# Strip runs of the value product that follow the groups of heads, in a transformer block on one core

## The chip, the cores and the metric

One core of one Trainium2 chip runs the whole kernel. The metric is device time in microseconds, as the median of several executions of the built program. Lower is better.

## The reference

The input is `x` of 2 x 1024 x 1024 (two sequences of 1024 tokens). Three sublayers follow each other, each with a layernorm without weights and a residual:

```python
x = x + 0.5 * ffn(layernorm(x))      # dense 1024x1024 + bias, 8 LoRA experts of rank 16, top 2
x = x + attn(layernorm(x))
x = x + 0.5 * ffn(layernorm(x))      # the same weights
```

The attention has 32 query heads and 8 key and value heads, each 32 wide, so four query heads share one key head; rotary positions; a causal mask; softmax; and an output projection:

```python
att   = einsum('bhgqd,bhkd->bhgqk', q, k) / sqrt(32)        # causal
probs = softmax(att)
ctx   = einsum('bhgqk,bhkd->bhgqd', probs, v)
out   = ctx @ Wo
```

All of it is in float32.

## The kernel before

The 2048 tokens are cut into 16 token tiles of 128, numbered 0 to 15; eight belong to each sequence. Token tile `t` attends to `L = t % 8 + 1` key tiles. The dense products are done in float16 halves (a high and a low part), three matmuls for each block of 128 rows. Each token tile passes four stages, written as Python generators: `a1` (first feed-forward), `a2` (keys, values, queries), `c1` (output projection, which reads the context) and `c2` (second feed-forward). The weights of `a2` and `c1` do not stay on the chip; they stream from DRAM into the three buffers `ws`, issued on SyncE's queue, and so do the transposing DMAs. `dense` (L362 to L364) holds the matmuls of all these stages: `pd<-ws` are `a2` and `c1`, `pd<-wb` and `misc<-ag` are the feed-forwards.

The attention goes through 128 pairs of a token tile and a group (four query heads with one key head). The token tiles come in the order 0 to 7, 9 to 15, and tile 8 (`LATE`) at the very end. For each pair:

- `unit_s1` computes the scores (L571) for each key tile, takes the row maximum on VectorE (L588), writes it into the queries as extra columns (L598, L599), and loads the queries again, transposed, by a DMA on SyncE's queue (`qt_load`, L554). This runs some pairs ahead (`LOOK`).
- `unit_s2` computes the transposed scores (L686) for each key tile, the exponential on ScalarE (L692) into a buffer `p32`, and for the diagonal key tile the mask on GpSimd (L694). Each such result is a unit, which it hands to `av_add`.
- `av_add` gathers units into a batch. A batch holds up to `BATCH` = 4 key tiles of one pair, and it is emitted once two further units (`SKEW`) are there.
- `av_batch` emits the batch: a strip run. For each unit there are 8 matmuls in float32: four heads, each with a stationary operand 32 columns wide at its own quarter of the array, once with the values (`va`) and once with ones, which gives the softmax's denominator. Each of the 8 appears twice in the profile. The result is in one PSUM buffer `av` (one buffer in all). At the last key tile of the pair the sums are copied out on ScalarE (L640, `o`), inverted and multiplied on VectorE (L642, L647), cast to the high half on ScalarE (L648), and the low half is taken on GpSimd (L649). High and low half are column blocks of the context tile, which `c1` reads as its stationary operand, blocks 0 to 7 in order.

So before, a pair with one to four key tiles is one run, and one with five to eight is a run of four and a run of the rest. The lines of the batching are

```python
if not pend or len(pend[-1][3]) == BATCH or pend[-1][0:2] != (t, g):
    pend.append((t, g, L, []))
```

A step for each token tile goes through its eight pairs and advances the dense stages of other tiles between the units, by sizes that are written out. The order in which instructions stand on each engine in the end is decided when the program is built, by a list scheduler with priorities. Within a run each matmul is tied to the one before it (`issue_after` with high priority), so nothing comes between them.

Of the kernel before, what the change touches and what calls it, by code (L numbers as in the profile page):

```python
# [9 lines left out]
FP = mybir.dt.float32  # L10
# [3 lines left out]
ALU = mybir.AluOpType  # L14
# [3 lines left out]
NH, NKV, DH, GRP = 32, 8, 32, 4  # L18
E, R = 8, 16
P = 128  # L20
KB = D // P
# [7 lines left out]
ATT = [t for t in range(NT) if t != LATE] + [LATE]  # L29
LOOK = [6, 6, 4, 4, 3, 3, 3, 3]  # L30
BATCH = 4
SKEW = 2
AHEAD = 5
NEARLY = 3
# [5 lines left out]
def kernel(  # L40
# [16 lines left out]
    nc = tc.nc  # L57
# [18 lines left out]
    p_av = ctx.enter_context(tc.tile_pool(name="p_av", bufs=1, space=bass.MemoryType.PSUM))  # L76
# [525 lines left out]
    pend = deque()  # L602
    ready = {}
    avt = [None]
# [12 lines left out]

    def av_batch():

        t, g, L, us = pend.popleft()  # L620
        if us[0][0] == 0:
            avt[0] = p_av.tile([P, 2, P], FP, name="av")
        av = avt[0]
        prev = None
        for n, (j, p32) in enumerate(reversed(us)):
            for i, w in enumerate((VA[t - t % TPB + j][:, g, :], ones)):
                for h in range(GRP):
                    rows = slice(h * DH, (h + 1) * DH)
                    with ExitStack() as st:
                        if prev is not None:  # L630
                            st.enter_context(tc.high_priority())
                            st.enter_context(tc.issue_after(prev.ins))
                        prev = nc.tensor.matmul(  # L633
                            av[rows, i, :], lhsT=w, rhs=p32[:, h, :],
                            start=(us[0][0] == 0 and n == 0 and i == 0), stop=(us[-1][0] == L - 1 and n == len(us) - 1),
                            skip_group_check=True, tile_position=(0, h * DH),
                        )
        if us[-1][0] == L - 1:
            o = pp.tile([P, 2, P], FP, name="o", bufs=2)
            nc.scalar.copy(o, av)  # L640
            rc = pp.tile([P, P], FP, name="rc", bufs=1)
            nc.vector.reciprocal(rc, o[:, 1, :])  # L642
            if t not in CTX:
                CTX[t] = Context()
            c = CTX[t]
            o2 = pp.tile([P, P], FP, name="o2", bufs=2)
            nc.vector.tensor_tensor(o2, o[:, 0, :], rc, ALU.mult)  # L647
            nc.scalar.copy(c.high(g), o2)  # L648
            nc.gpsimd.tensor_tensor(c.low(g), o2, c.high(g), ALU.subtract)  # L649
            if g == NKV - 1:  # L650
                CT[t] = CTX.pop(t)

    def av_add(t, g, j, L, p32):

        if not pend or len(pend[-1][3]) == BATCH or pend[-1][0:2] != (t, g):
            pend.append((t, g, L, []))
        pend[-1][3].append((j, p32))
        after = 0
        while len(pend) > 1:
            after = sum(len(b[3]) for b in list(pend)[1:])  # L660
            if after < SKEW:
                break
            av_batch()
# [15 lines left out]
    def unit_s2(t, g):  # L679
        b0 = t - t % TPB  # L680
        L = t - b0 + 1
        q = Ts.pop(("q2", t, g))
        cs = S["cs", g // 4]
        for j in range(L):
            ps = p_s2.tile([P, GRP, P], FP, name="s2")
            ins = nc.tensor.matmul(  # L686
                ps.rearrange("p h k -> p (h k)"), lhsT=KT[b0 + j][:, g, :],
                rhs=q.rearrange("p h k -> p (h k)"), start=True, stop=True,
            )
            s2_ins.append(ins.ins)  # L690
            p32 = pp.tile([P, GRP, P], FP, name="p32", bufs=8)
            nc.scalar.activation(p32, ps, AF.Exp, scale=cs)  # L692
            if j == L - 1:
                nc.gpsimd.affine_select(  # L694
                    out=p32, in_=p32, compare_op=ALU.is_ge, fill=0.0, base=0,
                    pattern=[[0, GRP], [1, P]], channel_multiplier=-1,
                )
            av_add(t, g, j, L, p32)
            yield

    def stage_c1(t):
        while t not in CT:
            av_batch()
        tt = CT.pop(t)
        xt = xts[t]
        for n in range(2):
            ps = p_dense.tile([P, 512], FP, name="pd")
            yield from dense_streamed(ps, tt, 3 + n)
            c = bass.ts(n, 512)
            nc.vector.scalar_tensor_tensor(xt[:, c], ps, S["uo", n], xt[:, c], ALU.mult, ALU.add)  # L710
            if n == 0:
                yield True
        Ts["x3", t] = layernorm(xt)
        yield True
# [94 lines left out]
    pp = ctx.enter_context(tc.tile_pool(name="pp", bufs=2, reuse_waits="tile"))  # L809
# [5 lines left out]
    def flush(_):  # L815
        while pend:
            av_batch()
        yield True
# [68 lines left out]
    def step(s):  # L887
# [26 lines left out]
        for g in range(NKV):  # L914
            u = pos + g + 1 + LOOK[t % TPB]
            if s == LATE - 1:
                u = min(u, LATE * NKV)
            if s == NT - 1 and g == 3:
                QS[LATE] = qst[LATE % 2]
                nc.sync.dma_start(out=QS[LATE], in_=late["q"])  # L920
            if u < len(units) and units[u][0] != t and s < NT - 1:
                while s != LATE - 1 and ready.get(units[u][0], 0) < (1 if units[u][1] < 4 else 2):
                    next(dn)
                    done += 1
            s1 = look(u)
            for _ in unit_s2(t, g):
                next(s1, None)
                slot += 1
                while done < npieces * slot / nslots:
                    next(dn, None)  # L930
                    done += 1
            for _ in s1:
                pass
# [73 lines left out]
```

## Time and profile before

| | us |
|---|---|
| median of 4 runs | 1524.83 |
| lowest, highest | 1523.23, 1526.64 |
| the profiled execution | 1523.23 |
| its span, first to last instruction | 1521.5 |

| engine | busy us | instructions |
|---|---|---|
| TensorE matmuls (PE) | 1428.3 | 16596 |
| TensorE weight loads (PEld) | 833.3 | 16596 |
| VectorE (DVE) | 1066.8 | 2396 |
| ScalarE (ACT) | 691.6 | 1280 |
| GpSimd (POOL) | 497.3 | 711 |

| stretch (us from the start) | transposed scores of token tiles |
|---|---|
| 152 to 307 | 0, 1, 2 (one to three key tiles) |
| 307 to 795 | 3 to 7 (four to eight) |
| 848 to 985 | 9, 10 (two, three) |
| 986 to 1442 | 11 to 15 (four to eight) |
| 1443 to 1470 | 8 (one) |

The first 150 us prepare the weights and begin the first feed-forwards. A row of the profile names the line, the engine, the operation and the tiles: `av<-p,va` writes `av` and reads `p32` and `va`. The matmuls overlap in the array, so their durations are longer than the distance of their starts; the distance is what counts where PE is the bound.

### The profile page before, as it was taken

To read this page: it belongs to the slowest core of one execution; us is meant where nothing else is said; L and a number is where in the kernel's file an instruction comes from. 1 tells how busy PE (TensorE), PEld (TensorE's weight loads), DVE (VectorE), ACT (ScalarE), POOL (GpSimd) and SP (SyncE) were. 2 spreads that over 40 slices of the span, in tenths; PEclk is the share of its full clock that TensorE was granted. 3 is DMA by queue.
4 is the path that set the end of the run, shared out by engine and by line. 5 is a ranking of instruction groups with operands and counts; after the bars stand their busy time and mean duration, and the time that the engine had idled before them with its cause. 6 is when DMAs were issued, how large, how long until landed. Compare 5 with 4: busy or idle time off the path is not lost.

```text
span 1521.5 us, 39480 instructions
## 1 busy us (share of the span) xinstructions
PE 1428.3 (94%) x16596; PEld 833.3 (55%) x16596; DVE 1066.8 (70%) x2396; ACT 691.6 (45%) x1280; POOL 497.3 (33%) x711
## 2 busy tenths in 40 slices
PE   3877989899999999999999898999999999999998
PEld 1433445556556566666654454555556566566543
DVE  6878666867768577776663756867877577776653
ACT  7444334544444454454550333444444455565520
POOL 3453342624324133232231433434333132231231
PEclk9998999999999999999999999999999999999999
DMA  9877796958494753646547769668594653663461
GB/s 279 290 204 203 166 276 188 225 148 239 103 249 90 211 170 78 237 114 146 185 119 245 187 157 251 187 178 228 96 266 87 201 169 78 209 140 78 123 190 43
DMA packets 297186, 267.57 MB, mean 176 GB/s; under 512 B 262576, under 2 KB 265648, under 8 KB 276528
## 3 DMA queue, kind: packets, MB, share of 16 engines
q1 hardware_dynamic: 293456, 252.47, 61.5%
q10 hardware_dynamic: 3552, 12.58, 2.2%
q8 instruction: 130, 2.13, 0.6%
q14 instruction: 48, 0.39, 0.1%
HBM read 181.63 MB, written 20.45 MB: 133 GB/s over the span
## 4 chain that ended last, share of the span: by engine, by line
PE 75%; DVE 10%; DMA 8%; issue 2%; POOL 2%; ACT 1%; SPq 1%; DVEq 0%; POOLq 0%; ACTq 0%
PE av L633 15%; PE pd L362 13%; PE pd L363 13%; PE pd L364 13%; PE s L571 8%; PE s L686 7%; DMA qt<-qst 3%; DMA ws<-wstr 2%; DVE ws L196 2%; DVE mx L588 1%; DVE hl L315 1%; DMA xt<-in_x_dram 1%; DMA tt<-hl 1%; PE pd L444 1%; PE pd L446 1%
## 5 line engine op out<-in xcount | busy, mean ns | idle before, releaser
L692 ACT ACTIVATE p<-s,cs 128x512 f32<-128x512 f32 x576 | 379.5, 687 | 281.8 <-PE s L686 278.9
L588 DVE TENSOR_REDUCE mx<-s 128x4 f32<-128x512 f32 x480 | 316.0, 676 | 162.6 <-PE s L571 149.6
L633 PE MATMUL av<-p,va 128*32 128x128 f32 x4608 | 237.0, 278 | 1.7 <-POOL p L694 1.0
L362 PE MATMUL pd<-ws,tt 128*128 128x512 f16 x592 | 226.3, 382 | 12.4 <-DMA ws<-wstr 8.5
L633 PE MATMUL av<-p,ones 128*32 128x128 f32 x4608 | 232.3, 273 | 0.0
L363 PE MATMUL pd<-ws,tt 128*128 128x512 f16 x592 | 225.9, 382 | 0.0
L364 PE MATMUL pd<-ws,tt 128*128 128x512 f16 x592 | 225.0, 381 | 0.0
L571 PE MATMUL s<-kts,qt 96*128 96x128 f16 x2304 | 200.0, 220 | 12.7 <-DMA qt<-qst 7.7
L686 PE MATMUL s<-qt,kts 128*128 128x512 f16 x576 | 201.1, 381 | 9.5 <-DMA qt<-qst 7.2
L363 PEld LDWEIGHTS <-tt 128*128 128x128 f16 x1360 | 134.2, 99 | 134.3 <-issue 16.9
L362 PEld LDWEIGHTS <-tt 128*128 128x128 f16 x1360 | 134.1, 99 | 134.2 <-DMA tt<-hl 12.1
L364 PEld LDWEIGHTS <-tt 128*128 128x128 f16 x1360 | 134.1, 99 | 128.8 <-issue 7.2
L571 PEld LDWEIGHTS <-qt 96*128 96x128 f16 x2304 | 151.4, 98 | 96.8 <-issue 35.7
L362 PE MATMUL pd<-wb,tt 128*128 128x512 f16 x512 | 195.5, 382 | 7.0 <-DMA tt<-hl 3.6
L363 PE MATMUL pd<-wb,tt 128*128 128x512 f16 x512 | 195.0, 381 | 1.5 <-DVE wb L196 1.5
L364 PE MATMUL pd<-wb,tt 128*128 128x512 f16 x512 | 195.0, 381 | 0.0
L633 PEld LDWEIGHTS av<-p,va 128*32 128x32 f32 x4608 | 122.5, 110 | 68.7 <-issue 58.9
L642 DVE RECIPROCAL rc<-o 128x128 f32<-128x128 f32 x128 | 121.1, 946 | 49.7 <-ACT o L640 49.5
L649 POOL TENSOR_TENSOR tt<-o,tt 128x128 f16<-128x128 f32 x128 | 55.7, 435 | 296.0 <-ACT tt L648 295.9
L694 POOL TENSOR_SCALAR_AFFINE_SELECT p<-p 128x512 f32<-128x512 f32 x128 | 84.5, 661 | 199.0 <-ACT p L692 199.0
L633 PEld LDWEIGHTS av<-p,ones 128*32 128x32 f32 x4608 | 138.4, 110 | 0.1
L583 POOL TENSOR_SCALAR_AFFINE_SELECT sm<-sm 128x512 f32<-128x512 f32 x96 | 62.9, 655 | 207.0 <-ACT sm L582 206.8
(175 smaller groups left out, 1798.1 us busy)
## 6 DMA issues: line engine op xcount, KB each, us to landing
ws<-wstr SPq DMA_DIRECT2D x148, 1024.0 KB, 5.6
wstr<-ws ACTq DMA_DIRECT2D x9, 1024.0 KB, 5.6
xt<-in_x_dram SPq DMA_DIRECT2D x16, 512.0 KB, 3.9
out_dram<-xt SPq DMA_DIRECT2D x15, 512.0 KB, 2.9
qt<-qst SPq DMA_TRANSPOSE x256, 3.0
ws<-in_wb_dram SPq DMA_DIRECT2D x2, 1024.0 KB, 8.8
qst<-in_wb_dram SPq DMA_DIRECT2D x2, 1024.0 KB, 7.5
st<-in_wo_dram SPq DMA_DIRECT2D x2, 1024.0 KB, 10.3
```

The lines of the kernel that those rows point to most:

```text
L362: nc.tensor.matmul(ps, lhsT=th, rhs=wh, start=(k == 0), stop=False)
L363: nc.tensor.matmul(ps, lhsT=th, rhs=wl, start=False, stop=False)
L364: nc.tensor.matmul(ps, lhsT=tl, rhs=wh, start=False, stop=(last and k == KB - 1))
L571: nc.tensor.matmul(ps[:, h, :], lhsT=q[0 : 3 * DH, h, :], rhs=KT[b0 + j][0 : 3 * DH, g, :], start=(not pem or h == 0), stop=not pem,)
L583: nc.gpsimd.affine_select(out=sm, in_=sm, compare_op=ALU.is_ge, fill=-3.0e38, base=0, pattern=[[0, GRP], [-1, P]], channel_multiplier=1,)
L588: nc.vector.tensor_reduce(mx[:, j, :], ps, AX.X, ALU.max)
L633: prev = nc.tensor.matmul(av[rows, i, :], lhsT=w, rhs=p32[:, h, :], start=(us[0][0] == 0 and n == 0 and i == 0), stop=(us[-1][0] == L - 1 ...
L642: nc.vector.reciprocal(rc, o[:, 1, :])
L649: nc.gpsimd.tensor_tensor(c.low(g), o2, c.high(g), ALU.subtract)
L686: ins = nc.tensor.matmul(ps.rearrange("p h k -> p (h k)"), lhsT=KT[b0 + j][:, g, :], rhs=q.rearrange("p h k -> p (h k)"), start=True, stop ...
L692: nc.scalar.activation(p32, ps, AF.Exp, scale=cs)
L694: nc.gpsimd.affine_select(out=p32, in_=p32, compare_op=ALU.is_ge, fill=0.0, base=0, pattern=[[0, GRP], [1, P]], channel_multiplier=-1,)
```

## The change

Batches may now hold units of two groups. With `L` up to `PAIRED` = 3 key tiles, an even group and the odd one after it go into one batch (two, four or six units), and both accumulate in one PSUM buffer, which is now one bank of 2 x 2 x 128 float32 columns. With `L` of 4 to `LONG` = 6, all key tiles of a group go into one batch. With 7 and 8 it stays at 4 and the rest. The evacuation is done once for each pair of groups where they share the bank: its instructions are then twice as wide. The buffers `o` and `rc` are twice as wide, `o2` is twice as wide with one buffer in place of two, and `p32` has ten buffers in place of eight.

```diff
+LONG = 6
+PAIRED = 3
...
-        t, g, L, us = pend.popleft()
-        if us[0][0] == 0:
-            avt[0] = p_av.tile([P, 2, P], FP, name="av")
+        t, g0, L, us = pend.popleft()
+        if us[0][1] == 0:
+            avt[0] = p_av.tile([P, 2, 2, P], FP, name="av")
         av = avt[0]
+        n = us[-1][0] - g0 + 1
+        last = us[-1][1] == L - 1
         prev = None
-        for n, (j, p32) in enumerate(reversed(us)):
+        for g, j, p32 in reversed(us):
             for i, w in enumerate((VA[t - t % TPB + j][:, g, :], ones)):
...
-                            av[rows, i, :], lhsT=w, rhs=p32[:, h, :],
-                            start=(us[0][0] == 0 and n == 0 and i == 0), stop=(us[-1][0] == L - 1 and n == len(us) - 1),
+                            av[rows, g - g0, i, :], lhsT=w, rhs=p32[:, h, :],
+                            start=(us[0][1] == 0 and (g, j) == us[-1][0:2] and i == 0), stop=(last and (g, j) == us[0][0:2]),
...
-        if us[-1][0] == L - 1:
-            o = pp.tile([P, 2, P], FP, name="o", bufs=2)
-            nc.scalar.copy(o, av)
-            rc = pp.tile([P, P], FP, name="rc", bufs=1)
-            nc.vector.reciprocal(rc, o[:, 1, :])
+        if last:
+            o = pp.tile([P, 2, 2, P], FP, name="o", bufs=2)[:, 0:n]
+            nc.scalar.copy(o, av[:, 0:n])
+            rc = pp.tile([P, 2, P], FP, name="rc", bufs=1)[:, 0:n]
+            nc.vector.reciprocal(rc, o[:, :, 1, :])
...
-            o2 = pp.tile([P, P], FP, name="o2", bufs=2)
-            nc.vector.tensor_tensor(o2, o[:, 0, :], rc, ALU.mult)
-            nc.scalar.copy(c.high(g), o2)
-            nc.gpsimd.tensor_tensor(c.low(g), o2, c.high(g), ALU.subtract)
-            if g == NKV - 1:
+            o2 = pp.tile([P, 2, P], FP, name="o2", bufs=1)[:, 0:n]
+            nc.vector.tensor_tensor(o2, o[:, :, 0, :], rc, ALU.mult)
+            hi, lo = c.tt[:, g0 : g0 + n, :], c.tt[:, KB + g0 : KB + g0 + n, :]
+            nc.scalar.copy(hi, o2)
+            nc.gpsimd.tensor_tensor(lo, o2, hi, ALU.subtract)
+            if us[-1][0] == NKV - 1:
                 CT[t] = CTX.pop(t)
...
-        if not pend or len(pend[-1][3]) == BATCH or pend[-1][0:2] != (t, g):
+        two = L <= PAIRED
+        fresh = not pend or (not two if pend[-1][0:2] != (t, g) else len(pend[-1][3]) == (BATCH if L > LONG else L))
+        if pend and two:
+            fresh = pend[-1][0] != t or (g % 2 == 0 and j == 0)
+        if fresh:
             pend.append((t, g, L, []))
-        pend[-1][3].append((j, p32))
+        pend[-1][3].append((g, j, p32))
...
-            p32 = pp.tile([P, GRP, P], FP, name="p32", bufs=8)
+            p32 = pp.tile([P, GRP, P], FP, name="p32", bufs=10)
```

## The prediction

> **What bounds the kernel now.** I read the page first: engine shares, then the chain.
>
> ```profile
> PE 1428.3 (94%) x16596; PEld 833.3 (55%) x16596; DVE 1066.8 (70%) x2396; ACT 691.6 (45%) x1280; POOL 497.3 (33%) x711
> ...
> PE 75%; DVE 10%; DMA 8%; issue 2%; POOL 2%; ACT 1%; SPq 1%; DVEq 0%; POOLq 0%; ACTq 0%
> ...
> L633 PE MATMUL av<-p,va 128*32 128x128 f32 x4608 | 237.0, 278 | 1.7 <-POOL p L694 1.0
> ```
>
> PE is the bound, and its strip matmuls (L633) wait for almost nothing. But the 94% is a mean, so I cut the span into stretches (length; busy us of PE, PEld, DVE, ACT and POOL with instructions; clock; DMA share; GB/s).
>
> ```profile
> 187.00:245.00 58.00, 51.17 (x506) 26.70 (x506) 37.51 (x97) 22.53 (x48) 20.84 (x31) 0.97 0.88 239
> 310.00:795.00 485.00, 484.70 (x6372) 296.83 (x6371) 347.97 (x760) 235.72 (x434) 146.86 (x210) 1.00 0.59 163
> 912.00:985.00 73.00, 66.38 (x709) 37.11 (x708) 54.34 (x113) 31.25 (x63) 29.99 (x40) 0.98 0.87 228
> 985.00:1424.00 439.00, 435.43 (x5928) 269.89 (x5927) 319.26 (x681) 221.03 (x406) 131.98 (x191) 1.00 0.59 155
> ```
>
> From 310 to 795 us, and nearly so from 985 to 1424, PE has no gap: there a saved PE nanosecond is a saved nanosecond. In the stretches of the short tokens (one to three key tiles) it lacks 7 us of 58 or 73, at 87% busy DMA: there waits set part of the pace.
>
> Then the timeline of PE around a strip run, first of one unit, then of four (start, duration).
>
> ```profile
> 1458.16 0.38 PE L686 MATMUL s<-qt,kts 128*128 128x512 f16 x1
> 1458.47 0.42 PE L633 MATMUL av<-p,va 128*32 128x128 f32 x8
> 1458.72 0.40 PE L633 MATMUL av<-p,ones 128*32 128x128 f32 x8
> 1459.05 0.40 PE L571 MATMUL s<-kts,qt 96*128 96x128 f16 x4
> ...
> 699.91 0.38 PE L364 MATMUL pd<-wb,tt 128*128 128x512 f16 x1
> 700.22 0.43 PE L633 MATMUL av<-p,va 128*32 128x128 f32 x8
> ...
> 702.10 0.40 PE L571 MATMUL s<-kts,qt 96*128 96x128 f16 x4
> ```
>
> Wide matmul to wide matmul, 0.89 us with one unit between, 2.19 with four. Three units cost 1.30, so one costs 0.434 to 0.437. Neighbouring wide matmuls start 0.216 apart. So 0.89 - 0.437 - 0.216 = 0.234 us belongs to no matmul: some 0.09 at the head and 0.14 at the tail, the price of entering and leaving the strip shape, the same for one unit as for four.
>
> **Part 1: fewer runs.** In the built programs' PE order I counted stretches of L633. Before 191: 32 of one unit, 32 of two, 30 of three, 96 of four, 1 of six. After 136: 8 of two, 16 of three, 72 of four, 16 of five, 24 of six. The matmuls are as many as before. 55 runs x 0.234 = 12.8 us of PE time. By place: 32 of the 55 belong to the tokens of five and six key tiles (16 per batch), which lie in the two stretches without gaps: 32 x 0.234 = 7.5 us, wholly on the path. The other 23, 5.4 us, belong to the tokens of one to three key tiles: 11 or 12 at 152 to 307 us, 7 or 8 at 848 to 985, 4 at 1443 to 1486.
>
> **Part 2: the wider evacuation.** 24 fewer each of L640, L642, L647, L648 and L649 (ACT and DVE lose 48 instructions each, POOL 24), hidden behind PE. But a pair's chain is longer. One group takes 371 + 946 + 348 + 297 + 435 ns = 2.4 us, with handovers about 2.8. For two groups the doubled DVE, ACT-cast and POOL rows and the nearest copy row (687, an ACT read of 128x512) give 0.69 + 1.89 + 0.70 + 0.59 + 0.87 = 4.7, with handovers 5.1; if width cost nothing it stays 2.8. I take 5, since reciprocal and subtract are long for their size. Who waits is the output projection of the same token, by the PE work that the new order puts between a token's last run and the first use of its context block 6: token 1 15 us, token 2 25, token 9 12, token 10 29, token 8 9: covered. Token 0 has 0.1 us: PE waits 4 to 5 us there. Before it waited at that spot too (0.80 for L648, then 1.72 for a weight load):
>
> ```profile
> 191.38 0.39 PE L362 MATMUL pd<-ws,tt 128*128 128x512 f16 x1 [0.80 <-ACT tt L648]
> ...
> 194.00 0.58 PE L362 MATMUL pd<-ws,tt 128*128 128x512 f16 x1 [1.72 <-DMA ws<-wstr]
> 194.38 0.63 PE L363 MATMUL pd<-ws,tt 128*128 128x512 f16 x1
> ```
>
> The last two rows show what a wait can cost beyond itself: the next starts are 0.38 to 0.43 apart, not 0.216, and the windows view has the clock at 0.50 for 193.84 to 197.25, that is 1.7 us lost. The clock is at 0.50 also at 876.5 and 934.5 (3.4 us each) and 286.0 (6.8 us); after the short wait at 1490.83 (0.63 us) it isn't.
>
> [...]
>
> So token 0's spot goes from 2.5 + 1.7 to about 4 + 1.7: +1.5. If the copy and reciprocal widen for nothing it is -2.
>
> **Part 3: the order around.** The scheduler moves wide work too. I summed PE rows between a group's last score matmul (L571) and its first transposed one (L686), between which lie the row maximum, two small DVE writes and a transposing DMA. In the trace the shortest such distance without a wait for the transposed queries is 5.1 us, and many take 8. After the change token 1's groups 1 to 3 have 2.6, 3.5 and 4.0 us of PE work (before 6.3, 9.8, 12.1) and token 9's group 2 has 3.1 (before 4.6). Token 0's wait above lies ahead of the first and swallows it; I take +1.5 for the rest of token 1 (a paired run also stands only 0.5 us behind its last scores) and +2 for token 9. Token 2 gains room (group 6: 5.7 to 9.6), where before had waits of 1.2 and 1.8: -1. Bounds for the part: -3 (all old waits gone) to +8 (each a full wait with its half clock).
>
> **Part 4: the end.** Token 8 runs last. Before, its output projection was through at 1490.0 and its second feed-forward began at 1503.79:
>
> ```profile
> 1489.60 0.59 PE L364 MATMUL pd<-ws,tt 128*128 128x512 f16 x2
> 1490.83 0.38 PE L362 MATMUL pd<-wb,tt 128*128 128x512 f16 x1 [0.63 <-DVE xt L710]
> ...
> 1503.79 0.23 PE L362 MATMUL misc<-ag,tt 128*128 128x136 f16 x1 [1.15 <-DMA tt<-hl]
> ```
>
> The 13.8 us between are a serial layernorm, split and transposing DMA, under 11.6 us of PE work of token 15. The new order leaves 7.8 us of work there. The chain shortens by one L710 (0.7) and one L335 (0.64), since the first half is done earlier: 12.5. So PE waits 4.7 us and may then run 3.4 us at half clock (1.7 more), against about 3.0 us of waits from 1483 on before. Net +3.4; bounds 0 (some of the old waits recur in neither) to +5.
>
> **Part 5: edits at nothing.** Ten weight buffers for eight: at most 9 units lie between first exponential and run's end in the new order (before 7 of 8), so no exponential waits for one. The single o2 buffer makes L647 wait for L649 of the run before; runs lie at least 1.6 us apart, mostly 5, and L649 follows L647 in about 1.2. The doubled reciprocal holds DVE 0.9 us longer in 24 places, ahead of L588, which frees the score banks; PE waited for L588 3.7 us in all before. I take 0; if each showed it would be 24 x 0.9 = 22. The one bank: PE waited for L640 0.6 us in the whole run.
>
> [...]
>
> **Sum.** -12.8 + 1.5 (token 0) + 1.5 (token 1) + 2 (token 9) - 1 (token 2) + 3.4 (end) = -5.4. The profiled execution took 1523.23 us (span 1521.5): 1517.8. It was the fastest of the four runs, 1.6 under the median 1524.83: 1519.4. As the old clock losses at 193.84 and 286.0 may go, I round down to 1519.
>
> **Rivals.** *The runs' time comes back whole* (no new waits, since the waits are on DMA and the stretches re-settle): 1524.83 - 12.8 = 1512. For it: the waits of before at 152 to 307 are as many as I add. Against: the 7.8 us left at the end are in the order. *Slower*: the pairs starve PE at the short tokens. Place: the 24 paired runs and the projections and scores behind them. Price: a wait of 2.3 us plus 1.7 of half clock, 4 each. From four such on it eats the 12.8, and six beyond my list give -5.4 + 24 = +18.6, so 1543; three give +6.6, 1531. Against: PE waited for L694 1.0 and for L640 0.6 us in all. *Nothing to measure* (0.2%, 3 us, is what a measurement of this kernel can tell): three or more of the 23 short-token gains lost and a hard end, 1522 to 1528. That the runs do not merge is ruled out by the order.
>
> **How the numbers follow.** Forecast (1514 to 1521.8) 0.56; whole gain (1510 to 1514) 0.18; nothing 0.15; slower 0.11. Faster is the first two: 0.74. The range takes in the whole gain's middle and the no-change case up to 1525.5, leaving out about 0.2.
>
> **What would show it.** In the profile after: PE busy less by 10 to 13 us; stretches of tokens 4, 5, 12 and 13 each shorter by 1.9; token 0's projection waiting for L648 or L649 about 4 us; an idle row of 4 to 5 us before the last L362 misc. Wrong: if the gap-free stretches don't shorten by 7.5 us in sum, if the half clock lasts beyond 25 us in all after 150 us, or if waits for L588 or L640 show in tens of us.

## The result and the profile after

The change made the kernel slower by a little: median 1527.23 us (53 runs) beside 1524.55 us for the kernel before (79 runs). The ratio is 1.0018, 95% interval 1.0012 to 1.0024, that is +2.7 us (1.8 to 3.7). The forecast was 1519 us, and "faster" at 0.74. The profiled execution took 1527.07 us, its span 1525.2; the one of the kernel before, 1523.23 us, was 1.3 us under its median. Three executions among those of the experiments took 1679, 3737 and 4266 us, and the ratios leave them out.

Lines after the change stand two to nine higher: L633 is now L637, L571 L573, L588 L590, L648 L653, L686 L695, L692 L701, L694 L703.

The page after: engine shares, the chain, and the row of the strip matmuls with its idle time.

```profile
PE 1423.5 (93%) x16596; PEld 845.5 (55%) x16596; DVE 1056.2 (69%) x2348; ACT 683.1 (45%) x1232; POOL 495.5 (32%) x687
...
PE 64%; DVE 14%; DMA 9%; POOL 5%; issue 4%; ACT 2%; SPq 1%; DVEq 0%; POOLq 0%; ACTq 0%
...
L637 PE MATMUL av<-p,va 128*32 128x128 f32 x4608 | 237.2, 278 | 5.6 <-POOL p L703 5.6
```

PE's busy time fell, but its share of the chain fell from 75% to 64%: more of the end is set by chains through VectorE, DMAs and GpSimd. The strip runs, which had waited 1.7 us in all, now wait 5.6 us for the mask.

The windows view, cut where the transposed scores of the first token of each stretch begin (tokens 0 to 2, 3 to 7, 9 and 10, 11 to 15, then 8 with the end; columns as in the prediction).

```profile
152.70:314.40 161.70, 142.62 (x1474) 82.22 (x1474) 110.11 (x245) 60.52 (x109) 59.88 (x78) 0.95 0.74 201
314.40:853.40 539.00, 533.79 (x6657) 323.90 (x6655) 368.96 (x807) 243.43 (x451) 164.11 (x225) 1.00 0.63 170
853.40:983.30 129.90, 120.93 (x1207) 68.48 (x1205) 94.02 (x219) 52.13 (x93) 48.58 (x66) 0.97 0.78 204
983.30:1444.60 461.30, 449.17 (x6233) 283.24 (x6231) 328.35 (x706) 229.61 (x422) 136.86 (x194) 1.00 0.57 153
1444.60:1521.00 76.40, 70.62 (x529) 35.99 (x526) 35.35 (x83) 14.57 (x30) 19.31 (x24) 0.98 0.39 111
```

The same cut of the kernel before and of one experiment (the changed kernel without its runs of six, told below), as length and PE's idle time (length minus PE busy):

| tokens | before | after | after, no runs of six |
|---|---|---|---|
| 0 to 2 | 155.0, 15.3 | 161.7, 19.1 | 160.9, 20.7 |
| 3 to 7 | 540.8, 1.4 | 539.0, 5.2 | 536.4, 1.9 |
| 9, 10 | 137.3, 11.8 | 129.9, 9.0 | 130.9, 8.9 |
| 11 to 15 | 457.6, 6.8 | 461.3, 12.1 | 459.3, 7.8 |
| 8 and the end | 73.9, 3.5 | 76.4, 5.8 | 75.8, 5.3 |
| sum | 1364.6, 38.9 | 1368.3, 51.2 | 1363.3, 44.6 |

Some work moves across the cuts between short and long tokens of a sequence (64 matmuls more in the first row). By whole sequences (rows one and two, three and four) the matmul counts agree within 4, and the first became 4.9 us longer, the second 3.7 shorter, the end 2.5 longer. The key is the two rows of the long tokens together, about 998 us with 8.2 us idle before. PE busy fell there by 7.2 us; some 2 us of this is work that now lies outside the cuts (16 matmuls fewer; an estimate from the distances of such matmuls' starts, 0.06 to 0.22 us). So about 5 us of the 7.5 forecast were saved. Idle time rose by 9.1.

Token 0's projection and the end, from PE's timeline, each with the windows row of the clock behind it (the column before the last two).

```profile
202.74 0.61 PE L364 MATMUL pd<-ws,tt 128*128 128x512 f16 x1 [4.31 <-ACT tt L653]
...
202.40:205.80 3.40, 3.06 (x14) 1.68 (x15) 0.28 (x1) 1.55 (x3) 0.89 (x2) 0.50 0.53 107
```

```profile
1506.02 0.23 PE L364 MATMUL misc<-ag,tt 128*128 128x136 f16 x1 [4.95 <-DMA tt<-hl]
...
1506.25:1509.65 3.40, 3.40 (x27) 2.75 (x24) 0.53 (x4) 0.57 (x2) 0.00 (x0) 0.50 0.07 29
```

These two waits came where and as long as the prediction put them, each with 3.4 us of half clock behind it (1.5 and 1.7 us lost).

New are small waits inside the stretches that had none. PE's waits from 480 to 620 us (tokens 5 and early 6; us in total, times, longest), first the changed kernel, then the one without runs of six:

```profile
PE pd L364 <- DMA ws<-wstr: 1.0, 2, 0.7
PE s L573 <- DVE mx L590: 0.8, 2, 0.6
PE s L573 <- DMA qt<-qst: 0.7, 1, 0.7
PE s L695 <- ACT p L701: 0.4, 2, 0.2
PE av L637 <- POOL p L703: 0.4, 1, 0.4
```

```profile
PE s L573 <- DVE mx L590: 0.6, 1, 0.6
```

What such a wait looks like, at the border of tokens 5 and 6: the timeline of PE and of ScalarE.

```profile
573.20 0.43 PE L637 MATMUL av<-p,va 128*32 128x128 f32 x8
...
575.96 0.62 PE L573 MATMUL s<-kts,qt 96*128 96x128 f16 x8
576.41 0.60 PE L695 MATMUL s<-qt,kts 128*128 128x512 f16 x2
...
578.36 0.38 PE L573 MATMUL s<-kts,qt 96*128 96x128 f16 x4 [0.17 <-DVE mx L590]
578.97 0.38 PE L695 MATMUL s<-qt,kts 128*128 128x512 f16 x1 [0.23 <-ACT p L701]
```

```profile
576.83 1.24 ACT L355 ACTIVATE xn<-xt,nb,rs 128x1024 f32<-128x1024 f32 x1 [3.17 <-DVE nb L350]
577.98 0.35 ACT L644 COPY o<-av 128x256 f32<-128x256 f32 x1
578.23 1.27 ACT L701 ACTIVATE p<-s,cs 128x512 f32<-128x512 f32 x2
```

For 2.76 us PE does nothing but the run, and no new score reaches ScalarE. Then PE gives out two score tiles and two transposed ones at once. But ScalarE's 3.17 us of idle time end with a layernorm row (L355) that waited for its statistics from VectorE (L350). This row of 1.24 us stands ahead in ScalarE's order; then come the copy of the run's sums and, only at 578.23, the two exponentials. There are two buffers for each kind of score, so PE has to wait. These rows do not tell the two causes apart, the bunch of scores and the layernorm row ahead of it: without runs of six, ScalarE at this border does two exponentials (577.50) before its layernorm row (579.22). At 1257 to 1262 us, the same border in the second sequence, the same rows recur.

### The profile page after: what moved, and what is told of

Read it like the earlier page. It is cut to its first block, busy times and chain, and to the rows that moved or that the text cites. A ratio compares the mean times of both kernels' runs of the same rounds, so it can differ in the third digit from the quotient of the medians.

```text
span 1525.2 us, 39320 instructions
## 1 busy us (share of the span) xinstructions
PE 1423.5 (93%) x16596; PEld 845.5 (55%) x16596; DVE 1056.2 (69%) x2348; ACT 683.1 (45%) x1232; POOL 495.5 (32%) x687
## 4 chain that ended last, share of the span: by engine, by line
PE 64%; DVE 14%; DMA 9%; POOL 5%; issue 4%; ACT 2%; SPq 1%; DVEq 0%; POOLq 0%; ACTq 0%
PE av L637 13%; PE pd L364 12%; PE pd L365 12%; PE pd L366 11%; PE s L573 7%; PE s L695 6%; DMA qt<-qst 3%; DMA ws<-wstr 3%; DVE mx L590 3%; DVE ws L198 2%; DVE hl L317 1%; POOL xt L401 1%; DVE bst L337 1%; DMA tt<-hl 1%; DVE rc L646 1%
## 5 line engine op out<-in xcount | busy, mean ns | idle before, releaser
L701 ACT ACTIVATE p<-s,cs 128x512 f32<-128x512 f32 x576 | 377.2, 688 | 250.3 <-PE s L695 246.7
L590 DVE TENSOR_REDUCE mx<-s 128x4 f32<-128x512 f32 x480 | 318.6, 678 | 215.6 <-PE s L573 193.6
L637 PE MATMUL av<-p,va 128*32 128x128 f32 x4608 | 237.2, 278 | 5.6 <-POOL p L703 5.6
L637 PE MATMUL av<-p,ones 128*32 128x128 f32 x4608 | 233.9, 275 | 0.0
L573 PE MATMUL s<-kts,qt 96*128 96x128 f16 x2304 | 199.4, 220 | 16.8 <-DMA qt<-qst 8.3
L365 PEld LDWEIGHTS <-tt 128*128 128x128 f16 x1360 | 134.4, 99 | 136.5 <-issue 12.1
L573 PEld LDWEIGHTS <-qt 96*128 96x128 f16 x2304 | 153.0, 98 | 102.5 <-issue 35.3
L695 PE MATMUL s<-qt,kts 128*128 128x512 f16 x576 | 195.9, 381 | 4.6 <-ACT p L701 2.3
L637 PEld LDWEIGHTS av<-p,va 128*32 128x32 f32 x4608 | 128.0, 110 | 48.7 <-issue 34.3
L703 POOL TENSOR_SCALAR_AFFINE_SELECT p<-p 128x512 f32<-128x512 f32 x128 | 85.7, 670 | 197.8 <-ACT p L701 197.6
L637 PEld LDWEIGHTS av<-p,ones 128*32 128x32 f32 x4608 | 139.4, 111 | 0.2
L646 DVE RECIPROCAL rc<-o 128x128 f32<-128x128 f32 (+1 forms) x104 | 117.4, 1129 | 29.2 <-ACT o L644 29.1
L654 POOL TENSOR_TENSOR tt<-o,tt 128x128 f16<-128x128 f32 (+1 forms) x104 | 55.1, 530 | 253.6 <-ACT tt L653 253.5
```

Of the source, the lines that this page charges most:

```text
L365: nc.tensor.matmul(ps, lhsT=th, rhs=wl, start=False, stop=False)
L573: nc.tensor.matmul(ps[:, h, :], lhsT=q[0 : 3 * DH, h, :], rhs=KT[b0 + j][0 : 3 * DH, g, :], start=(not pem or h == 0), stop=not pem,)
L590: nc.vector.tensor_reduce(mx[:, j, :], ps, AX.X, ALU.max)
L637: prev = nc.tensor.matmul(av[rows, g - g0, i, :], lhsT=w, rhs=p32[:, h, :], start=(us[0][1] == 0 and (g, j) == us[-1][0:2] and i == 0), st ...
L646: nc.vector.reciprocal(rc, o[:, :, 1, :])
L654: nc.gpsimd.tensor_tensor(lo, o2, hi, ALU.subtract)
```

## The experiments

All but one are cut from the changed kernel. The diffs show what differs from it. Each ratio is to the kernel before, run beside it. Differences in us are (ratio - 1) x 1524.5; the interval of each is about ±2 us, ±3 for the runs of three and of seven.

**Runs of five alone, and runs of five and six, without pairs.**

```diff
-LONG = 6
-PAIRED = 3
+LONG = 5
+PAIRED = 0
```

> Only the tokens of five key tiles change: all five in one run in place of 4 + 1; no pairs. 175 runs in place of 191. Theory A (a run's entry and exit, 0.234 us, is really saved, and what the change lost are new waits at the tokens of one, two and six key tiles): 16 x 0.234 = 3.7 us less than before, and no waits over 0.1 us in the stretches of tokens 4 and 12. Theory B (the saving is never collected, because PE then waits for something else everywhere): 0. Theory C (any change of the order moves the time by a few us at random): anywhere from -4 to +4.

Measured: 1520.85 us, ratio 0.9981 (0.9966 to 0.9996), -2.9 us: near theory A, though theory C's span holds it too. PE waits for nothing at token 4 and 0.3 us at token 12 (0.7 before). The trace, of the slowest of the 12 executions (1525.97 us), doesn't show the gain: its two rows of the long tokens take 998.4 us as before, with 3.1 us less PE busy and 3.1 more idle.

```diff
-PAIRED = 3
+PAIRED = 0
```

> Runs of five and of six, no pairs. 159 runs. Theory A: -7.5 from 32 runs, plus the waits of the changed kernel in the stretches of tokens 5 and 13 (3.9 and 4.9 us there, none before): about +1 against before, and about 4.5 us slower than the kernel with runs of five alone. Theory B: 0 and no difference between the two. Theory C: no pattern.

Measured: 1528.42 us, ratio 1.0028 (1.0016 to 1.0040), +4.3 us. The only difference between the two is that 16 pairs have one run of six in place of four and two. That saves 16 runs and costs 7 us more. By the row prices it should have saved 3.7; with the waits already seen in the changed kernel, theory A had put it 4.5 us above the fives. One chain of it, from GpSimd's and PE's timelines:

```profile
545.23 3.50 POOL L401 TENSOR_TENSOR xt<-xt,bb 128x512 f32<-128x512 f32 x2
548.68 0.64 POOL L585 TENSOR_SCALAR_AFFINE_SELECT sm<-sm 128x512 f32<-128x512 f32 x1
...
556.64 0.39 PE L695 MATMUL s<-qt,kts 128*128 128x512 f16 x1 [1.71 <-DMA qt<-qst]
```

A mask of scores stood behind two bias additions; the row maximum, the DMA of the queries and the transposed scores behind it came late. This suggested GpSimd's queue as the cause, which the last pair of runs tries.

**Pairs alone, and without those of the tokens of one key tile.**

```diff
-LONG = 6
+LONG = 4
```

> Pairs of groups for tokens of one to three key tiles, nothing else (runs of up to four as before otherwise). 168 runs. Theory A: -5.4 from 23 runs, plus the new waits of the changed kernel at tokens 0, 1 and 8 (token 0's projection 4.3, half clock 5 more, the end 3.3, less what token 9 and 2 gain): +4 to +6, so 0 to +2 us in all; the waits of 4 to 5 us for L653 near 200 us and for the transposed split near 1500 us stand in the trace. Theory B: 0. Theory C: no pattern, and these two waits not at those places.

Measured: 1526.55 us, ratio 1.0008 (0.9996 to 1.0020), +1.2 us, as expected; 0 (theory B) is inside the interval too. The two waits stand in the trace where theory A put them (4.3 us for L653, 4.9 before the last feed-forward), which speaks against C.

```diff
-LONG = 6
+LONG = 4
...
-        two = L <= PAIRED
+        two = 2 <= L <= PAIRED
```

> Pairs only for tokens of two and three key tiles; tokens 0 and 8 as before. 176 runs. Theory A: -3.5 from 15 runs; the wait near 200 us for token 0's context and the 5 us wait before the last feed-forward are gone, so -1 to -4 against before, and 1 to 5 us faster than the kernel with all pairs. Theory B: 0. Theory C: no pattern.

Measured: 1529.83 us, ratio 1.0030 (1.0018 to 1.0042), +4.6 us: a miss. The wait for token 0's context fell from 4.3 to 0.8 us and the one before the last feed-forward from 4.9 to 1.1, both as expected, but at token 2 new waits stand that neither kernel had. From PE's timeline, and from its waits between 260 and 300 us:

```profile
270.63 1.03 PE L573 MATMUL s<-kts,qt 96*128 96x128 f16 x8 [3.27 <-DMA qt<-qst]
```

```profile
PE s L695 <- DMA qt<-qst: 4.4, 1, 4.4
```

Undoing the two parts I had priced as losses made the kernel slower: near the short tokens what an edit does is not its own price, but where the whole order lands.

**Runs of five, with pairs in some tokens.**

```diff
-LONG = 6
+LONG = 5
...
-        two = L <= PAIRED
+        two = t in (9, 10)
```

> Runs of five, and pairs only for tokens 9 and 10. 167 runs in place of 191. Theory A, put together from the stretches (each stretch's loss or gain belongs to its own tokens): -3.7 from the fives; tokens 9 and 10 took 137.3 us before and 130.2 with pairs, token 11 after them 2.4 more, so -4.7; in all about -8 against before, with no wait for token 0's context and no 5 us wait at the end. Rival (the short tokens' waits are settled by the whole order, and not by their own stretch): no better than the fives alone, -3.

Measured: 1519.22 us, ratio 0.9963 (0.9948 to 0.9978), -5.6 us, the middle between the two expectations. It is the fastest version found and beats both kernels.

```diff
-LONG = 6
+LONG = 5
...
-        two = L <= PAIRED
+        two = L <= PAIRED and t != LATE
```

> Fives, and pairs for all short tokens but the last one (token 8). 156 runs. Theory A: the fives alone gave -2.9 to -4, all pairs +1.5, and the end without pairs gets 2.5 to 3.3 back: -4 to -6 against before, and the wait before the last feed-forward 1.2 us again instead of 5. Token 0's wait of 4.3 us stays. Rival: the end is settled elsewhere, -2.

Measured: 1521.30 us, ratio 0.9984 (0.9968 to 1.0000), -2.4 us: the rival's value, though both waits are as theory A said (4.3 us at token 0, 1.1 before the last feed-forward). By the medians the pairs of tokens 0 to 2 take back 3.2 us of the 5.6, about as much as the ±3 us of such a difference; the two traces do not show it (1363.9 us from token 0's first transposed score to the end, 1365.0 without these pairs).

**The changed kernel without runs of six.**

```diff
-LONG = 6
+LONG = 5
```

> The changed kernel with the sixes cut to four and two as before, the pairs and the fives kept. If the parts add up: the fives alone gave -4.2 us and the pairs alone +1.2, so -3 us, 1521 to 1522 beside 1524.5 (ratio 0.998). Rival, the short tokens' stretches are settled by the whole order and not by the part: anything from -6 to +2 us.

Measured: 1523.92 us, ratio 0.9995 (0.9981 to 1.0009), -0.8 us, inside the rival's span and 2.2 us above the sum, which lies just outside the interval. It is the last column of the table above. Against it the runs of six in the changed kernel cost 3.5 us; in the two stretches of long tokens they save 3.0 us of PE time and bring 7.6 us of idle time. (The trace without them is of its fastest execution, 1520.25 us.)

**Is it the length of the run?** The pairs of six key tiles as two runs of three (as many runs as before, another order), and the pairs of seven as one run of seven (no pairs in both, fives kept):

```diff
-PAIRED = 3
+PAIRED = 0
...
-len(pend[-1][3]) == (BATCH if L > LONG else L))
+len(pend[-1][3]) == {5: 5, 6: 3}.get(L, BATCH))
```

> Fives, and the six key tiles in two runs of three instead of four and two: as many runs as the kernel with fives alone (175), another order. If it is the length of the run that brings the waits at the tokens of six (it can't be parted, so the scores behind it come in a bunch): no waits over 0.5 us in their stretches and the same time as with the fives alone (-3 against before). If any other order at these tokens brings waits: 3 to 5 us of them in each of the two stretches, and 4 to 8 us slower than the fives alone.

Measured: 1526.86 us, ratio 1.0013 (0.9993 to 1.0032), +2.0 us. That is 4.9 us above the fives, inside the 4 to 8 of "any other order", and speaks against the length alone. The same kernel once more, for its trace:

> The kernel of the run before it (five key tiles in one run of five, six in two runs of three), once more, for its waits. If any other order at the tokens of six key tiles brings waits, the waits of TensorE in the stretches of tokens 5 and 13 come to 3 us or more in each (none in the kernel before, 3.2 and 3.9 with one run of six). If only the length of the run does it, they are below 1 us in each.

Measured: 1525.07 us, one execution. Its waits are neither below 1 us nor above 3 in both. Between a token's first transposed score and the next token's, PE waits 0 us at token 5 and 2.0 at token 13, where the fives alone already wait 1.4; with runs of six it is 2.3 and 3.0 in the changed kernel. So in these traces the waits of token 5 come only with the run of six; at token 13 the order brings some by itself. From token 0's first transposed score to the end it takes 1368.5 us, like the fives alone (1369.4, their slowest execution) and the kernel before (1369.1). Why the median of this kernel lies some 5 us above that of the fives stays open.

```diff
-PAIRED = 3
+PAIRED = 0
...
-len(pend[-1][3]) == (BATCH if L > LONG else L))
+len(pend[-1][3]) == {5: 5, 7: 7}.get(L, BATCH))
...
-p32 = pp.tile([P, GRP, P], FP, name="p32", bufs=10)
+p32 = pp.tile([P, GRP, P], FP, name="p32", bufs=11)
```

(`o`, `rc` and `o2` are one group wide here.)

> Fives, and the seven key tiles in one run (eleven weight buffers): 159 runs, 3.7 us less of entries and exits than the fives alone. In the built order the PE work between a group's last score and its transposed score falls to 3.5 to 6 us at token 14 (8 to 11 before) and 7 to 12 at token 6. Theory of the long run: waits of 1 to 2 us for the transposed queries at token 14 and 6 in a good part of the groups, 6 to 12 us in all, so 2 to 8 us slower than the fives alone. If only six is unlucky: 3.7 us faster than the fives alone.

Measured: 1542.46 us, ratio 1.0124 (1.0102 to 1.0146), +18.9 us, that is 21.8 above the fives: the expectation was right in sign, far too small in size. From its waits of PE:

```profile
PE s L695 <- DMA qt<-qst: 23.3, 15, 3.7
```

Before, that wait was 7.2 us in six times, all at tokens 0 to 2. Here it is 8.0 us there, 3.7 at token 6, 3.3 at token 7, none at token 14 and 8.2 at token 15: so one of the two tokens forecast, and the two of eight key tiles that follow them. In the stretches of the long tokens it is nil with runs of five and in the changed kernel, 4.7 us with runs of six and no pairs, and 15.2 here.

**Is it GpSimd's queue?** Both kernels with the bias addition cut to 16 of each 512 columns, which leaves most of the bias out:

```diff
-            c = bass.ts(n, 512)
+            c = slice(512 * n, 512 * n + 16)
             nc.gpsimd.tensor_tensor(xt[:, c], xt[:, c], bb[:, c], ALU.add)
```

> The kernel before with the bias addition on GpSimd cut to 16 of each 512 columns (so most of the bias is left out): 64 additions of 1.7 us shrink to about 0.15 us each, and the order on the engines stays nearly as it was. Theory: GpSimd's queue, in which a mask or a copy of the row maximum stands behind two additions of 3.4 us, is what turns the new order's shorter distances into waits. Then this kernel gains little, 0 to 6 us, since the order before had few such waits (POOL p 1.0 us, row maximum 3.7 us).

Measured on the kernel before: 1511.38 us, ratio 0.9918 (0.9903 to 0.9933), -12.5 us, twice what was expected. The shrunk additions take 0.47 us in the mean, not 0.15. In the traces, which are 9.2 us apart, nearly all of it lies ahead of token 0, which begins at 143.4 us in place of 152.4:

```profile
143.40:1507.80 1364.40, 1327.05 (x16073) 782.81 (x16071) 902.54 (x2094) 609.96 (x1148) 367.00 (x608) 0.99 0.63 168
```

From there on it takes 1364.4 us beside 1364.6 (both cut 4.4 to 4.5 us before the end): in these traces, cutting GpSimd's additions gained nothing in the part that the change touches.

> The changed kernel with the bias addition on GpSimd cut in the same way. Theory (GpSimd's queue makes the waits): it gains 8 to 13 us and comes to lie 5 to 9 us under the kernel before with the same cut, about as I had first predicted. Rival (the distances in the order alone, whatever stands in GpSimd's queue): it gains what the other gains, and stays within 3 us of it or above.

Measured on the changed kernel: 1516.90 us, ratio 0.9943 (0.9926 to 0.9959), -8.7 us. Against the changed kernel it gained 11.4 us, inside the theory's 8 to 13, but the other gained 12.5; what tells them apart is where it lies, and that is 3.8 us above the kernel before with the same cut, as the rival said. The theory that GpSimd's queue makes the loss falls. With most of the additions gone, PE waits for weights and for queries instead, which were 8.6 and 7.7 us in the kernel before with the same cut (PE's waits in the whole run):

```profile
PE pd L364 <- DMA ws<-wstr: 15.5, 10, 3.2
PE s L695 <- DMA qt<-qst: 10.3, 4, 7.3
```

## Why the prediction was wrong

The experiments split the change into parts. A measured term is the difference of two kernels' ratios to the kernel before, good to about ±3 us (±2 for fives and sixes). The terms form one chain of kernels, so their sum is the whole by construction. The column of the traces is the same difference in one profiled execution each, from token 0's first transposed score to the end (1369.1 us in the kernel before).

| part | runs saved | forecast us | measured us | in the traces | from |
|---|---|---|---|---|---|
| fives | 16 | -3.7 | -2.9 | +0.3 | fives alone |
| sixes | 16 | -3.7 | +3.5 | +4.6 | changed kernel against the one without sixes |
| pairs of 9, 10 | 8 | +0.1 | -2.7 | -4.3 | fives with those pairs against fives alone |
| pairs of 0 to 2 | 11 | -0.6 | +3.2 | -1.2 | all pairs but token 8's against pairs of 9, 10 |
| pairs of 8 | 4 | +2.5 | +1.6 | +4.0 | all pairs against all but token 8's |
| sum | 55 | -5.4 | +2.7 | +3.4 | |

The sixes are the part that stands clear: without pairs they cost 7.2 us by the medians and 5.2 in the traces.

**The step that failed** is in Part 1: "32 x 0.234 = 7.5 us, wholly on the path". It took the gap-free stretches as a place where a saved PE nanosecond is a saved nanosecond. PE did save time there, but a gap-free stretch says only that no wait showed with the order as it was, not that the other engines had room to spare. By the medians the sixteen fives kept most of their gain (-2.9 us, between -0.6 and -5.2; their one trace shows none). The sixteen sixes missed theirs by 7.2 us; the sum was wrong by 8.1, and the errors of the other parts nearly cancel. A run of six holds PE for 2.76 us, in which no score comes out; then scores come out in a bunch, with two buffers for each kind, and ScalarE and VectorE serve them in turn. Most of the waits that are new are 0.2 to 0.7 us long, and they have different releasers: late row maximum, exponential, mask, queries, weights. That merging four and two into six brings the loss is shown by two pairs of kernels whose code differs in nothing else (+3.5 and +7.2 us). Why it does is argued from the rows: which part is the run's length and which the order that the scheduler makes around it is only partly settled, by the runs of three (another order alone: 4.9 us above the fives) and of seven.

**Part 3** had the wrong waits. For tokens 0 to 2 I took +0.5 (+1.5 - 1) and looked only at the way from scores to transposed scores. The waits for the queries, which I priced, in fact shrank from 7.7 to 2.0 us between 152 and 314 us. Two others came, one for streamed weights and one at the mask of the units themselves, from PE's and GpSimd's timelines:

```profile
186.06 0.61 PE L364 MATMUL pd<-ws,tt 128*128 128x512 f16 x1 [5.02 <-DMA ws<-wstr]
```

```profile
290.41 2.49 POOL L401 TENSOR_TENSOR xt<-xt,bb 128x512 f32<-128x512 f32 x2
292.85 1.62 POOL L703 TENSOR_SCALAR_AFFINE_SELECT p<-p 128x512 f32<-128x512 f32 x1
...
295.47 0.68 POOL L703 TENSOR_SCALAR_AFFINE_SELECT p<-p 128x512 f32<-128x512 f32 x1
...
296.21 0.66 PE L637 MATMUL av<-p,va 128*32 128x128 f32 x8 [3.40 <-POOL p L703]
```

The weights' three loads were issued from 176.80 us on, behind four loads of queries; before, single ones went out at 171.88 and 175.81, and PE waited 3.1 us there in two pieces. The four kernels with pairs at tokens 0 to 2 and the whole bias addition all have this wait in one piece (2.9 to 5.0 us). The half clock behind it in the changed kernel (185.3 to 188.7) stands in no term.

A run takes its units in reverse, the masked one first, so in a pair of token 2 one late mask holds back six units. The clock is at half from 294.5 to 301.3, so that the run behind the wait takes 5.31 us in place of 2.76: 6 us lost at one place. It is not 6 us more than before: token 2 had 6.8 us of half clock before too and 6.1 us of idle time, against 5.0 now. Nor is it GpSimd's additions alone: with them cut, the changed kernel waits 8.3 us for queries at token 2. Whether the pairs of tokens 0 to 2 miss their forecast at all stays open, since the medians and the traces disagree. For token 9 I took +2 where nothing was lost: by the medians pairs of 9 and 10 gained 2.7.

**What was right.** The run's price: in the rows at 573 us a run of six takes 2.76 us to the next matmul, that is 12 groups 0.218 apart and 0.14 at the tail, as in the kernel before. (0.89 - 0.437 - 0.216 is 0.237 and not 0.234; that moves the sum by 0.2 us.) Part 2: 4.31 us of wait at token 0's projection, forecast 4; the second wait of 1.72 us, which I kept, has gone, but the wait of 5.02 us for weights stands ahead of it; the five wide operations took 0.58 + 1.74 + 0.49 + 0.41 + 0.73 = 3.95 us, 0.8 less than taken. Part 4: 4.95 us before the last feed-forward, forecast 4.7; the part with its four runs measured +1.6 against +2.5. Part 5: PE's waits for the row maximum rose from 3.7 to 6.9 us, but not in the rows of tokens 0 to 2 and 9, 10, where the evacuation is wide (2.3 before, 2.2 after), and none for L644 shows. So the wide evacuation and the single bank cost next to nothing of their own, and the 22 us did not come. One thing was luck: the pairs together came to +2.1 us by the medians where the terms gave +2.0, because their errors (-2.8, +3.8, -0.9) cancel.

**The marks that I had set.** Two of those for "wrong" came: the gap-free stretches did not shorten by 7.5 us in sum (they grew by 1.9), and the half clock after 150 us lasts 27 us in all, above the 25 named and the 17 of before. PE busy fell by 4.8 us where 10 to 13 were said. The stretches of tokens 4, 5, 12 and 13, from first transposed score to first transposed score, changed by +0.3, +0.6, -1.0 and +0.2 us where each was to lose 1.9. From token 0 on PE busy fell by 8.6 (1325.7 to 1317.1), with 10 us more at half clock in it, and ahead of token 0 it rose by 3.9 at a lower mean clock (0.91 to 0.88).

**The rivals.** The slower one had its place at the pairs, with waits of 4 us each; the pairs together lost 2.1 us by the table, and the loss that decided lay at the sixes, for which I had no rival at all. "Nothing to measure" (1522 to 1528) had the number, but by another way, the short tokens and a hard end; the loss is small, and its interval leaves zero out.

## What to carry to other kernels

An engine without gaps has its speed from the others' keeping up (the long tokens' 998 us had 8.2 us of PE idle time before, 17.3 after): before a saving there is taken in full, ask how long the longer undivided block keeps the producers and consumers around it idle, and whether banks and queues can take the bunch that follows. Cut such a change into its parts by place, since here five key tiles in a run and pairs in two tokens gain 5.6 us together while the same edit a step further loses them. Near waits that already set the pace, a sum over edits can't be relied on, because a list scheduler moves the rest (taking back two parts priced as losses made the kernel 3.4 us slower); only a run of each order tells, by the median of several executions: the differences between two single traces lie up to 4.4 us from those of the medians here.

## What the runs showed of the hardware

VectorE's subtraction of the low half (`hl<-xn,hl`, 128x1024) takes 1.25 us in the mean where no bias addition of GpSimd runs beside it (21 times in the kernel before) and 2.08 us where one does (27 times). With the additions cut to 16 columns it is 1.29 us in all 48, and VectorE is busy 50 us less (1015.4 beside 1065.4 us up to the last cut). So beside such a row the subtraction took 0.83 us longer; what in such a row makes it longer is not shown. GpSimd's row itself (L399) is 1.74 us in the mean for 128x512 (1.26 at the least), against 0.74 us for VectorE's three-operand row of that size (L447).

TensorE's clock went to half in the changed kernel at 212.60 us after waits of 0.16, 0.73 and 0.56 us only; PE was busy in 1.97 of the 3.42 us before. In the kernel before it went to half at 193.84 us, after waits of 0.80 and 1.72 us, and after the one wait of 0.63 us at 1490.83 it did not. The clock also stayed at half while PE was busy: the strip run at 296.21 us went at half speed for 5.1 us without a gap, after a wait of 3.4 us, and the clock was back at 301.35. This half clock, from 294.52 us on, lasted 6.83 us, those from 202.40 and 1506.25 us 3.40 each; what sets these lengths is not shown.
